# Four-layer conditioned sequence kernel: when the first batch's q and k, the heads' means, the first gates and the matrix exponential's pieces are issued

## The chip, the cores and the metric

One core of a Trainium2 chip. The metric is the device time of one execution in microseconds (us); the time of the kernel before is the median of 3 runs. Engines: TensorE (PE, with its weight loads PEld), VectorE (DVE), ScalarE (ACT), GpSimd (POOL) and SyncE (SP), which issues nearly all DMAs.

## The reference

Input x is 32 x 128 x 144 in float32, with a condition of 144 numbers for each of the 32 batches. Four layers follow one another:

- Layer L0 is a transformer block. From the condition come six vectors (shift, scale and gate, for attention and for the MLP). x is normalised, scaled and shifted; q, k and v are projected; **q and k are normalised over the 9 numbers of each of the 16 heads** (mean removed, divided by the root of the variance, times a gain); then softmax attention, projection, gated residual, and a gated MLP with gelu.
- Layer L1 rotates x in a 64-dimensional subspace: U comes from a QR factorisation of P (144 x 64), and the rotation is **the matrix exponential of a skew matrix** (64 x 64) that depends on the condition, one for each batch.
- Layer L2 is a transformer block as L0, without the normalisation of q and k.
- Layer L3 is one with a mixture of four experts, of which two are taken for each token.

```
qkv = xn @ w_qkv + b_qkv
...
q = _ln(q, g_q)
k = _ln(k, g_k)
attn = softmax(einsum('bhqd,bhkd->bhqk', q, k) * HD ** (-0.5))
...
U, _ = qr(P)
R = expm(A)
x_rot = x + einsum('btd,nd->btn', z @ R - z, U)
```

## The kernel before, in words

The kernel is written with the order of every engine's instructions given by hand. Time is cut into **ticks**; a tick is the work on one batch of 128 tokens in each of three stages. `at_tick` gives each batch of the three transformer layers its tick: batch b of L0 is at tick b, and layers L2 and L3 follow. In a tick the loop issues the scores of the current batch twice over (half the heads each, `scores`, L853), the exponentials of the batch before, and the weighting, division and projection of the batch before that (`weigh` L880, `sums`, `divide`, `project_out` L944). Between them lie named gaps, in this order: a, e, t, (scores, first half), stats, b0, b, den, pre1, (scores, second half), c, y1, y2, y3, d, z. `put(tick, gap, f, ...)` hangs other work into a gap, and `fill` issues it. A gap's work is issued in the order in which it was put there. Every engine takes its instructions in this order, so what waits holds up all that is behind it on that engine.

Ticks -6 to -1 are the lead-in: nothing is scored yet. What hangs in them and in the ticks of L0:

- `modulations(n)` (L274 to L281): 80 small matmuls and four DVE copies that make shifts and scales of layer n. `layer_gates(n)` (L291 to L298): eight matmuls, one ACT copy and two DMA writes of the gates to DRAM, from where `load_gates` (L305) reads them back for four batches at a time. `first_gates` is `layer_gates(0)` followed by two DMA loads of L3's modulation weights, over those of L0.
- `ln_stats` (L623 to L635): statistics of a batch on DVE and the normalised batch on POOL; `ln_T` (L652 to L655): its transposes on PE and the modulation on ACT.
- `qk0_project` (L686 and L687, ACT copies L741 and L742), `qk0_variance` (DVE L747, POOL L748), `qk0_guess` (DVE L754 and L757), three `qk0_newton` (L764 to L767: four small instructions, on POOL, for batch 0 on DVE), `qk0_divide` (DVE L771) and `qk0_T` (PE L783, ACT L786 to L788): q and k of one batch of L0. Batch i has its projection at tick i - 3, guess and Newton steps at i - 2, division and transposes at i - 1.
- `without_means` (L1166 to L1172): seven DVE instructions that take the mean over a head out of the weights of q and k once, so that the projection gives q and k without means.
- `prep_qr`: 64 columns of a Householder QR, three pieces each (PE L327, ACT L338 and L340, POOL L339; DVE L342 to L349; DVE L353). `prepare_qr` issues three pieces in a tick before 0 (e, then twice in stats) and six after it (a, twice in t, den, y1, y2): columns 6 and 7 fall into tick 0, 8 and 9 into tick 1.
- `prep_expm`: the exponential, cut into 50 pieces by `yield`: two pieces of modulations and gates for L2 and L3; four that make the skew matrices (L414, L420, L429, L434; the first of them issues four more loads of the weights W, L189); four for the norm and the number of squarings (L444 to L482); eight products for the powers (L501); two series of ten; two products; eight squarings (L561, L567); a branch L586 for more squarings, which is not taken here; a last subtraction (L592). `prepare_expm` issues one piece at the end of gap z of tick -2, and from tick 0 on one in b and one in z.
- When the QR and the exponential are done, `prep_rot` (L601) makes the rotations, and `load_late` issues the loads of the later layers' weights.

Of the kernel before, what the change touches and what calls it, by code (L numbers as in the profile page):

```python
# [66 lines left out]
def tile_kernel(ctx: ExitStack, tc: tile.TileContext, a: dict, out: bass.AP):  # L67
    nc = tc.nc
# [721 lines left out]
    def values(g, i0, n, rest_first=False):  # L790
        p = PARAMS[g[0]]
        if g[0] == 0:
            ps = by_token0(g, i0, n, p.wv, p.wvR, f"ps_v_{g[1]}")
            pss, copy = [ps.rearrange("p b c -> p (b c)")], nc.scalar.copy
        else:
            pss = yield from by_token(g, "a", i0, n, p.wv, p.wvR, f"ps_v_{g[0]}_{g[1]}", rest_first)
            copy = nc.vector.tensor_copy
        pair = take_v()
        for i in range(n):
            st[g[0] * B + g[1] * G + i0 + i]["v"] = pair[:, i * NH : (i + 1) * NH, :]  # L800

        m = 8 * n // len(pss)
        for i, ps in enumerate(pss):
            v = pair[:, 2 * m * i : 2 * m * (i + 1), :].rearrange("p (q r) s -> p q (r s)", r=2)
            src = ps.rearrange("p (q r d) -> p q r d", r=2, d=HD)
            copy(v[:, :, :HD], src[:, :, 0, :])
            copy(v[:, :, 48 : 48 + HD], src[:, :, 1, :])
# [353 lines left out]
    prep_qr, prep_expm = prep_qr(), prep_expm()  # L1161
# [41 lines left out]

    def prepare_expm(tick, gap):
        nonlocal prep_expm
        if prep_expm and (tick >= 0 and gap in ("b", "z") or (tick, gap) == (-2, "z")):
            said = next(prep_expm, 0)
            if said == 0:
                prep_expm = None
            elif said is not None:  # L1210
                rot_T.append(said)


    GAP = 3
    first = (0, B + GAP, 2 * B + GAP)
    at_tick = {first[l] + b: l * B + b for l in range(3) for b in range(B)}
# [3 lines left out]
    def put(tick, gap, f, *args):  # L1220
        gaps[tick, gap].append((f, args))

    def put2(tick, gap, to, f, *args):

        halves = []

        def first_half():
            halves.append(f(*args))
            next(halves[0])

        def second_half():
            for _ in halves[0]:
                pass

        put(tick, gap, first_half)
        put(tick, to, second_half)

    for layer in range(3):
        ahead = 5 if layer == 0 else 6
        for n in range(NG):  # L1240
            g = (layer, n)
            t0 = first[layer] + n * G
            for i in range(G):
                s = layer * B + n * G + i
                at_a = t0 + i - ahead
                if layer == 1 and n == 0:
                    at_a = t0 - 4 + i // 2
                if layer == 1 and i == 0:
                    put(at_a - 2, "d", rotate_T, n)
                    put(at_a - 1, "b", rotate_in, n)  # L1250
                    put(at_a - 1, "d", rotate, n)
                stats[at_a].append((s, "a"))
                stats[t0 + i + 3].insert(0, (s, "m"))
                if layer < 2:
                    put(*((at_a, "d") if at_a != t0 + i - ahead else (at_a + 1, "b")), ln_T, s, "a")
                else:
                    put(at_a, "d", ln_T, s, "a")
                if layer == 0:
                    put(t0 + i + 4, "a", ln_T, s, "m")
                else:  # L1260
                    put(t0 + i + 3, "d", ln_T, s, "m")
                if layer == 0:
                    put(t0 + i - 3, "c", qk0_project, s)
                    put(t0 + i - 3, "z", qk0_variance, s)
                    put(t0 + i - 2, "e", qk0_guess, s)
                    if s == 0:
                        for gap in "bbc":
                            put(-2, gap, qk0_newton, s, nc.vector)
                    else:
                        for gap in ("b", "c", "y2"):  # L1270
                            put(t0 + i - 2, gap, qk0_newton, s)
                    put(t0 + i - 1, "b", qk0_divide, s)
                    put(t0 + i - 1, "c", qk0_T, s)
            if layer == 0:
                for i in (0, 2):
                    put(t0 + i // 2, "b", lambda g=g, i=i: list(values(g, i, 2)))
            elif layer == 1:
                put2(t0, "stats", "b", values, g, 0, 2, True)
                put2(t0 + 1, "stats", "b", values, g, 2, 2, True)
            else:  # L1280
                put2(t0, "y2", "y2", values, g, 0, 2, True)
                put2(t0 + 1, "den", "pre1", values, g, 2, 2)
            if layer:
                put2(t0 - 2, "c", "c", qk_chunks, g)
                if g == (1, 0):
                    put(t0 - 2, "y2", qk_masked, g)
                for r in (1, 0):
                    if layer == 2 and n > 2:
                        for t in range(2):
                            put(t0 - 2 + (r == 0), "z", qk_mask, g, nc.gpsimd, t, r)  # L1290
                    elif g != (1, 0):
                        put(t0 - 1, "a", qk_mask, g, nc.gpsimd, 0, r)
                        put(t0 - 1, "b0", qk_mask, g, nc.scalar, 1, r)
            if layer == 0:
                put2(t0 + 10, "stats", "b", mlp1, g, 0, (0, 1, 2), True)
                put2(t0 + 11, "d", "d", mlp1, g, 3, (3, SHARED), False)
                for i in range(G):
                    put(t0 + 12 + i // 2, "bd"[i % 2], mlp2, g, i)
            elif layer == 1:
                put2(t0 + 8, "c", "c", mlp1, g, 0, (0, 1, 2), True)  # L1300
                put2(t0 + 9, "c", "c", mlp1, g, 3, (3, SHARED), True)
                for i in range(G):
                    put(t0 + (10, 10, 11, 11)[i], "bdbc"[i], mlp2, g, i)
            else:
                put2(t0 + 7, "den", "c", gate_logits, g)
                put(t0 + 8, "e", expert_ranks, g)
                put(t0 + 8, "stats", expert_weights, g)
                for i in range(G):
                    put(t0 + 8 + i // 2, "cdab"[i], moe_bias, g, i)
                for pair in range(2):  # L1310
                    at_ = t0 + 8 + 2 * pair
                    put2(at_, "stats", "b0", moe1, g, pair, 0, True)
                    put2(at_, "den", "pre1", moe1, g, pair, 1, False)
                    put2(at_ + 1, "stats", "b0", moe1, g, pair, 2, True)
                    put2(at_, "stats", "y1", shared_by_gate, g, pair)
                    put2(at_, "y2", "y3", moe2_parts, g, 2 * pair, 0)
                    put(at_ + 1, "b", moe2, g, 2 * pair, 1)
                    put(at_ + 1, "c", moe2, g, 2 * pair, 2)
                    put(at_ + 1, "y2", moe2, g, 2 * pair, 3)
                    for i in range(G):  # L1320
                        put(at_ + 2, "aabb"[i], moe2, g, 2 * pair + 1, i)
                put(t0 + 12, "b", moe_out, g)

    put(-5, "b", modulations, 0)
    put(-4, "b", first_gates)
    put(-4, "z", without_means)

    put(first[1] + B - 10, "c", load_L3)
    put(first[1] + B + 7, "d", lambda: load_pair(1, mlps[:, :PAIR_COLS]))
# [1 line left out]
    def fill(tick, gap):  # L1331
        prepare_qr(tick, gap)
        while (tick, gap) == (last_prep, "b0") and late is None:
            prepare_qr(tick, gap)
            prepare_expm(tick, gap)

        if gap == ("t" if tick < 0 else "e" if tick < first[1] else "stats") and tick in stats:
            ln_stats(stats.pop(tick))
        for f, args in gaps.pop((tick, gap), ()):
            f(*args)  # L1340
        prepare_expm(tick, gap)
# [213 lines left out]
```

## Time and profile before

| | us |
|---|---|
| median of 3 runs | 1320.95 (1320.02 to 1337.16) |
| the profiled execution's own time | 1327.05 |
| its span | 1325.3 |
| busy: PE, DVE, ACT, POOL | 1266.7, 799.8, 832.9, 699.9 |
| first scores (tick 0) begin | 40.88 |
| tick 3 begins | 72.77 |
| tick 25 begins | 336.25 |
| late weights are issued from | 395.23 |

Rows of the timeline read: start, duration, engine, line, operation, what is written and read, the shape, how many of the same are merged in the row; in brackets how long the engine stood idle before, and what released it. The table by stretches gives the busy time of PE, PEld, DVE, ACT and POOL in each, then the granted clock of TensorE (1 is full), then the DMA share and GB/s. A pass over a float32 matmul is two instructions, so a count of 2 is one product.

### The profile page before, as it was taken

The numbers are of one execution on the slowest core, as the hardware profiler recorded it, in microseconds if no ns is written. First come the engines' busy times: TensorE is split into PE (matmuls) and PEld (weight loads), VectorE is DVE, ScalarE is ACT, GpSimd is POOL, SyncE is SP. The second block draws the span as 40 slices with busy tenths as digits, with TensorE's granted clock in tenths as the row PEclk, the third lists the DMA queues.
The fourth block names the chain that finished last, engine by engine and source line by source line (L and its number), as shares of the span: only waits on it lengthen the run. The fifth ranks groups of instructions, "written<-read, shape, count | busy, mean of one in ns | idle before, by whom it ended". The sixth has DMA issues, their size and how long they took to land.

```text
span 1325.3 us, 35652 instructions
## 1 busy us (share of the span) xinstructions
PE 1266.7 (96%) x14180; PEld 923.5 (70%) x14180; DVE 799.8 (60%) x2516; ACT 832.9 (63%) x1832; POOL 699.9 (53%) x1691
## 2 busy tenths in 40 slices
PE   6989898999999989999999999999999999999997
PEld 5668686786776566677776766667676767677665
DVE  5698988866764355666566667545454546455322
ACT  2568767678767555686767777756565656555431
POOL 5667777756744343445445445736363636351632
PEclk9999999999999999999999999999999999999999
DMA  9200000000003000000110000201000000000000
GB/s 229 61 2 21 20 3 18 20 3 22 20 13 121 18 11 20 11 20 10 45 29 14 17 20 11 75 11 19 10 19 11 19 11 19 10 19 2 19 9 9
DMA packets 21671, 34.43 MB, mean 26 GB/s; under 512 B 2304, under 2 KB 12448, under 8 KB 21248
## 3 DMA queue, kind: packets, MB, share of 16 engines
q1 hardware_dynamic: 20848, 31.70, 8.0%
q8 instruction: 114, 1.87, 0.6%
q10 hardware_dynamic: 656, 0.42, 0.2%
q14 instruction: 53, 0.43, 0.1%
HBM read 29.65 MB, written 2.47 MB: 24 GB/s over the span
## 4 chain that ended last, share of the span: by engine, by line
PE 69%; DVE 4%; ACT 1%; issue 1%; POOL 0%; POOLq 0%; DVEq 0%
PE ps_h L665 19%; PE ps_f L1105 9%; PE ps_s L853 6%; PE ps_qk L665 6%; PE ps_o L880 5%; PE ps_w L853 5%; PE ps_f L970 4%; PE ps_pj L944 3%; PE ps_v L665 2%; DVE nm L858 2%; PE ps_f L1110 1%; PE ps_o L812 1%; PE ps_cw L1093 1%; PE ps_hT_m L652 1%; PE ps_hT_m L653 1%; PE ps_z L1002 1%
## 5 line engine op out<-in xcount | busy, mean ns | idle before, releaser
L858 DVE TENSOR_REDUCE nm<-ps_s 128x4 f32<-128x512 f32 x384 | 246.4, 682 | 96.9 <-PE ps_w L853 79.3
L865 ACT ACTIVATE pr<-ps_w 128x512 f32<-128x512 f32 x384 | 208.6, 595 | 107.6 <-PE ps_w L853 106.0
L853 PE MATMUL ps_w<-q,kT 32*128 32x128 f32 x3072 | 228.6, 283 | 0.2 <-ACT hid L964 0.2
L853 PE MATMUL ps_s<-kT,qT 32*128 32x256 f32 x1536 | 227.9, 404 | 0.7 <-ACT kT L788 0.6
L853 PEld LDWEIGHTS ps_w<-q,kT 32*128 32x128 f32 x3072 | 193.3, 186 | 9.7 <-issue 6.2
L964 ACT ACTIVATE hid<-ps_h 128x512 f32<-128x512 f32 (+1 forms) x224 | 119.1, 591 | 108.9 <-PE ps_h L665 108.5
L853 PEld LDWEIGHTS ps_s<-kT,qT 32*128 32x128 f32 x1536 | 134.9, 184 | 30.0 <-issue 9.2
L665 PE MATMUL ps_h<-hM_m,mlps 128*128 128x512 f32 x304 | 146.3, 615 | 0.0
L1114 DVE SCALAR_TENSOR_TENSOR acc<-ps_f,cw,acc 128x144 f32<-128x144 f32 x128 | 46.6, 366 | 152.3 <-PE ps_f L1110 73.6
L930 POOL TENSOR_TENSOR x_sb<-x_sb,res_a 128x144 f32<-128x144 f32 x96 | 47.0, 489 | 151.2 <-DVE res_a L933 149.9
L880 PE MATMUL ps_o<-pr,vaug 128*32 128x128 f32 x3072 | 104.9, 277 | 0.8 <-issue 0.8
L880 PEld LDWEIGHTS ps_o<-pr,vaug 128*32 128x32 f32 x3072 | 78.7, 110 | 34.3 <-PE ps_w L853 20.0
L665 PEld LDWEIGHTS ps_h<-hM_m,mlps 128*128 128x128 f32 x304 | 53.9, 191 | 66.2 <-issue 65.0
L731 POOL TENSOR_SCALAR kT<-kT,cst 128x512 f32<-128x512 f32 x40 | 62.3, 1563 | 61.6 <-ACT kT L718 60.6
L970 PE MATMUL ps_f<-mlps,hid 128*128 128x144 f32 x640 | 93.2, 293 | 0.0
L970 PEld LDWEIGHTS ps_f<-mlps,hid 128*128 128x128 f32 x640 | 82.5, 191 | 7.3 <-issue 3.4
L865 ACT ACT_TABLE_LOAD x57 | 73.1, 1283 | 8.0 <-PE ps_w L853 7.2
L626 POOL TENSOR_SCALAR rs_m_a<-mv_m_a 128x2 f32<-128x2 f32 x81 | 15.5, 191 | 116.6 <-DVE mv_m_a L624 88.2
L655 ACT ACTIVATE hM_m<-ps_hT_m,modM 128x128 f32<-128x128 f32 x96 | 44.6, 465 | 49.1 <-PE ps_hT_m L653 49.0
L961 ACT ACT_TABLE_LOAD x58 | 74.4, 1283 | 1.0
L930 POOL TENSOR_TENSOR x_sb<-x_sb,res_m 128x144 f32<-128x144 f32 x64 | 32.3, 510 | 80.0 <-DVE res_m L933 79.9
L1105 PEld LDWEIGHTS ps_f<-pair,hid 128*128 128x128 f32 x512 | 66.9, 190 | 8.4 <-issue 7.7
(324 smaller groups left out, 2963.5 us busy)
## 6 DMA issues: line engine op xcount, KB each, us to landing
gates<-gates SPq DMA_DIRECT2D x48, 288.0 KB, 3.5
x_sb<-in_x SPq DMA_DIRECT2D x8, 288.0 KB, 9.4
out_x<-x_sb SPq DMA_DIRECT2D x8, 288.0 KB, 2.5
mlps<-in_L_mlp SPq DMA_DIRECT2D x2, 1000.0 KB, 6.1
pair<-in_L_mlp SPq DMA_DIRECT2D x1, 1800.0 KB, 9.5
mlps<-in_L_mlp SPq DMA_DIRECT2D x1, 1800.0 KB, 8.2
pow<-in_W SPq DMA_DIRECT2D x4, 320.0 KB, 7.7
mlps<-in_L_wmod SPq DMA_DIRECT2D x4, 290.0 KB, 4.9
```

The source lines that it names most:

```text
L665: nc.tensor.matmul(ps, x, y, start=k == 0, stop=k == 1)
L731: eng.tensor_scalar(o, k, m, None, ALU.mult)
L853: nc.tensor.matmul(o, x, y, start=True, stop=True)
L858: nc.vector.tensor_reduce(nmv[:, at0 : at0 + 2, ONE : ONE + 2], view.rearrange("p (r t k) -> p r t k", t=2, k=T), AX.X, ALU.max, negate=True,)
L865: nc.scalar.activation(pr[:, 4 * e : 4 * e + 4, :].rearrange("p s q -> p (s q)"), view, AF.Exp, scale=SCALE,)
L880: nc.tensor.matmul(po[rows4(j), t, :], v[:, 4 * j + 2 * t + r, :], prs[j // 2][:, 4 * (j % 2) + 2 * r + t, :], start=r == 0, stop=r == 1,)
L930: nc.gpsimd.tensor_tensor(x_sb[:, b, :], x_sb[:, b, :], t, ALU.add)
L961: nc.scalar.activation(t, half, AF.Gelu_apprx_tanh)
L964: nc.scalar.activation(hid[:n, i], ps[:n], AF.Gelu_apprx_tanh)
L970: nc.tensor.matmul(ps, hid[:, at0, i, :], w2[:, m, :], start=m == 0, stop=m == NFC - 1)
L1105: nc.tensor.matmul(ps[:, 0, :], hid[:, at0 + m, i, :], w2[:, at0 + m, :], start=m == 0, stop=m == 3)
L1114: nc.vector.scalar_tensor_tensor(acc, ps[:, 0, :], w, acc, ALU.mult, ALU.add)
```

## The change

Batch 0's projection, variance, guess, Newton steps, division and transposes are each put one tick earlier (the transposes go before the other work of gap b of tick -2; the division into gap z of tick -3); those of the other batches stay. `without_means` goes from gap z of tick -4 to gap t of tick -5, after the first batch's statistics. `first_gates` goes from gap b of tick -4 to gap b0 of tick -2. The exponential's first piece is no longer issued at tick -2, nor the next ones in ticks 0 to 2: all begin at tick 3, two in a tick as before.

```
-        if prep_expm and (tick >= 0 and gap in ("b", "z") or (tick, gap) == (-2, "z")):
+        if prep_expm and tick >= FIRST_EXPM and gap in ("b", "z"):
...
+    FIRST_EXPM = 3
...
                 if layer == 0:
-                    put(t0 + i - 3, "c", qk0_project, s)
-                    put(t0 + i - 3, "z", qk0_variance, s)
-                    put(t0 + i - 2, "e", qk0_guess, s)
-                    if s == 0:
+                    early = s == 0
+                    put(t0 + i - 3 - early, "c", qk0_project, s)
+                    put(t0 + i - 3 - early, "z", qk0_variance, s)
+                    put(t0 + i - 2 - early, "e", qk0_guess, s)
+                    if early:
                         for gap in "bbc":
-                            put(-2, gap, qk0_newton, s, nc.vector)
+                            put(-3, gap, qk0_newton, s, nc.vector)
+                        put(-3, "z", qk0_divide, s)
+                        put(-2, "b0", first_gates)
+                        put(-2, "b", qk0_T, s)
                     else:
                         for gap in ("b", "c", "y2"):
                             put(t0 + i - 2, gap, qk0_newton, s)
-                    put(t0 + i - 1, "b", qk0_divide, s)
-                    put(t0 + i - 1, "c", qk0_T, s)
+                        put(t0 + i - 1, "b", qk0_divide, s)
+                        put(t0 + i - 1, "c", qk0_T, s)
...
     put(-5, "b", modulations, 0)
-    put(-4, "b", first_gates)
-    put(-4, "z", without_means)
+    put(-5, "t", without_means)
```

## The prediction

> **What bounds the kernel now.** I read the page's shares and slices, then the timeline of TensorE (PE) over the lead-in, then VectorE (DVE) over ticks 0 to 2, then the clock by stretches, then PE around tick 22.
>
> ```profile
> PE 1266.7 (96%) x14180; PEld 923.5 (70%) x14180; DVE 799.8 (60%) x2516; ACT 832.9 (63%) x1832; POOL 699.9 (53%) x1691
> PE   6989898999999989999999999999999999999997
> ```
> PE is busy 96% of the span; only the first of 40 slices (33 us each) stands at 6 tenths. Work can be moved, but PE's time can only shrink where it is idle or its clock is low.
>
> ```profile
> 16.86 2.13 PE L291 MATMUL ps_gate<-mlps,csT 72*32 72x144 f32 x8
> 24.95 1.17 PE L686 MATMUL ps_qk<-L_wqk,hM_a 128*128 128x288 f32 x2
> 37.46 1.09 PE L783 MATMUL ps_qkT<-cst,qkn 128*128 128x128 f32 x4 [3.01 <-DVE qkn L771]
> 40.88 1.55 PE L853 MATMUL ps_s<-kT,qT 32*128 32x256 f32 x8
> 43.66 2.56 PE L274 MATMUL ps_mod<-csT,mlps 72*128 72x32 f32 x74
> 49.14 0.65 PE L686 MATMUL ps_qk<-L_wqk,hM_a 128*128 128x288 f32 x2
> ```
> Columns: start, duration, engine, line, what, idle before it. The first scores come at 40.88, after 3.01 us of waiting for batch 0's division. The same 288-column pair takes 1.17 us before 41 us and 0.65 us after it: the lead-in runs at about half the clock. From 26.87 to 33.25 PE works on the exponential's first piece (modulations and gates of layer 1), 6.4 us at that speed.
>
> ```profile
> 42.67 0.16 DVE L342 SCALAR_TENSOR_TENSOR ala<-qrr,qr 128x1 uint32<-128x1 uint32 x1 [0.23 <-POOL qr L339]
> 53.96 0.16 DVE L342 SCALAR_TENSOR_TENSOR ala<-qrr,qr 128x1 uint32<-128x1 uint32 x1 [0.80 <-POOL qr L339]
> 64.37 0.16 DVE L342 SCALAR_TENSOR_TENSOR ala<-qrr,qr 128x1 uint32<-128x1 uint32 x1 [1.89 <-POOL qr L339]
> 75.44 0.15 DVE L342 SCALAR_TENSOR_TENSOR ala<-qrr,qr 128x1 uint32<-128x1 uint32 x1
> ```
> These four are the first QR column of ticks 0, 1, 2 and 3 on DVE, so those ticks last 11.29, 10.41 and 11.07 us.
>
> ```profile
> 76.00:80.00 4.00, 2.80 (x30) 2.18 (x31) 3.65 (x14) 1.34 (x6) 3.64 (x11) 0.91 0.00 0
> 80.00:84.00 4.00, 3.82 (x16) 2.40 (x14) 3.83 (x15) 2.38 (x6) 2.23 (x9) 0.66 0.00 0
> ```
> Third from the end is the granted clock: it drops after PE stood idle for 1.77 us before 77.20.
>
> ```profile
> 298.10 0.48 PE L853 MATMUL ps_s<-kT,qT 32*128 32x256 f32 x2
> 304.41 1.16 PE L561 MATMUL ps_sq<-pow 64*64 64x64 f32 x64
> 323.60 0.73 PE L944 MATMUL ps_pj<-L_wproj,oT 128*128 128x144 f32 x4 [1.24 <-PEq L586]
> 336.25 0.48 PE L853 MATMUL ps_s<-kT,qT 32*128 32x256 f32 x2
> 346.70 0.48 PE L853 MATMUL ps_s<-kT,qT 32*128 32x256 f32 x2
> 358.70 0.48 PE L853 MATMUL ps_s<-kT,qT 32*128 32x256 f32 x2
> ```
> Tick 22 starts at 298.10, tick 25 at 336.25, 26 at 346.70, 27 at 358.70. The exponential is over in tick 24 (its last subtraction is at 330.1), so ticks 25 to 27 run without pieces: 10.45, 12.0 and 11.4 us. The branch L586 costs PE 1.24 us.
>
> **The change part by part.** 50 pieces (a 51st call ends the generator) now run one at tick -2 and two per tick from 0; afterwards two per tick from 3, ending at 28.
>
> *Means (tick -4 to -5).* Seven DVE instructions from 19.33 to 21.71, 2.38 us. They now start at about 10.9, after the first statistics; their weights, issued at 3.34 and 4.29, landed 5.9 and 5.3 us later. QR column 1 on DVE slips from 12.53 to 13.3 and ends at 15.1. Cost nothing: PE is in the first modulations until 15.73. Without that cover it is 0.8 us.
>
> *Gates (tick -4 to -2).* Eight matmuls, 2.13 us on PE, one ACT copy of 0.39, two DMA writes and two weight loads on SP. SP is busy with x loads until 25.44 and writes the gates at 25.56 now; later it is about 27.5, and the loads about 29 instead of 26.87. The first reader, the gates' load issued at 34.56, has until tick 2; the weights until tick 3. On PE they fall into a wait for DVE. Nothing, or 2.1 us where PE was not waiting.
>
> *Batch 0's q and k.* Batch 0's h is ready at 17.87, so the projection runs 17.7 to 19.85 instead of 20.70 to 23.19, its variance is done on DVE at 21.1. Guess, QR column 3 (to 24.1), three Newton steps (0.88 each, as from 27.57 to 30.1 now) and division end at 27.2 instead of 37.3. Queued behind them on DVE is QR column 4: 27.75 instead of 25.90. PE: gates to 26.9, transposes 27.3, projection of batch 1 28.6 to 30.7, column 5, projection of batch 2 to 33.7. Column 5 ends on DVE at 35.0, and scores could start at 35.7 instead of 40.88. But POOL is next: batch 1's three Newton steps (1.30 us each, as from 37.46 to 41.28 now) start at 35.3 and end at 39.2, and the root of column 6 is queued behind them. DVE's column 6 thus comes at 40.5 instead of 42.67. Gain 2.2 us; ends: 0 (if POOL starts no earlier) and 5.2 (scores' own gain).
>
> *Ticks 0 to 2 lose their pieces.* Tick 0 sheds 3.5 us of modulations (43.66 to 47.14) and 1.85 us of W on PE; what stays on PE is 6.4 us. DVE stays busy 8.5, 8.5 and 8.0 us, less 0.9 of copies, 1.05, and 1.05 with the 1.21 row sum. With the QR chain's wait of 0.5 to 1 us I take 8.8 us a tick: 26.5 against 32.77, gain 6.3. Ends: 8 us (DVE alone, 8.2 a tick) and 2 us (10.3 a tick, with PE at half clock for a good half of each).
>
> *Clock.* PE stands idle in these ticks now, about 2 us each. The row says 1.77 us idle cost a stretch in which the clock lost 0.09 and 0.34 of 4 us, 1.7 us. One such drop: +1.5; ends 0 and 4 (a drop in nearly every tick).
> [...]
>
> *The pieces in ticks 3 to 28.* Seven pieces that ran before tick 3 now run in it or later: on PE 3.48 twice, 1.85, 1.16, 2.7, 1.16, together 13.8 us. I laid each tick's new pair on a tick of the same phase. Ticks 3 to 7: PE or DVE sets 14.5, 11.9, 11.5, 11.6 and 10.5 us against 12.52, 10.63, 10.47, 9.55 and 9.47, that is +7.3. Ticks 8 to 24: pairs change places among alike ones, -1.3. Ticks 25 to 27: squarings as in ticks 21 and 22 (12.95 and 13.30) and the branch, against 10.45, 12.0 and 11.4: +2.5, +1.3, +1.2. Sum 11.0. Ends: 8 (PE's idle time in ticks 25 to 28, about 5 us, takes them) and 14 (all of it on the path).
>
> *Branch.* L586 moves from the end of tick 23 to the middle of tick 27, where PE is further ahead of DVE; queued behind it are values, scores and all the rest of the tick. +1; ends 0 and 3.
>
> **Sum.** -2.2 - 6.3 + 1.5 + 11.0 + 1.0 = +5.0 us. The profiled execution took 1327.05 (span 1325.3 and 1.75 around it), so its like would take 1332; it stood 6.1 above the median of the runs shown, 1320.95. On that median: **1326 us**.
>
> **Rivals.**
> *The filler costs nothing later.* The pieces of ticks 25 to 28 and 3 to 7 run in idle time: the last sum is 8 less 1, the branch 0, the clock 0: -8.5 + 7 = -1.5, and with DVE-bound ticks 0 to 2 (8 us) and the scores' 5.2: -6. Time 1315 to 1320. For: PE idles 2.7 us in tick 28 and 2.1 in tick 3. Against: tick 25 has PE busy for all of its 10.45.
> *Half clock through ticks 0 to 2.* Speaks for it: the lead-in's 9 us of unbroken PE work from 23.88 to 33.25 did not lift the clock, and the ticks after hold less work. At half clock 6.5 us of work a tick become 13: 39 against 32.77 is +6.2 where I counted -4.8; sum +16, 1337. Against: the clock did lift at about 42.
> *Slower by over 2%.* The exponential outlives the QR tail, and the late weights, issued from 395.23, come late. It now ends at tick 28; the QR tail ends there too, so one piece more begins to delay. A squaring in a row costs about 3.6 us (PE, ACT and PE again), so from eight such pieces on it is over 26 us. Count from the row at 330.1: none is left. 1350.
> *Nothing moves at the head.* POOL's Newton steps hold column 6 at 42.67: +2.2 more, 1328.
>
> **How the numbers follow.** Forecast 0.53 (its own range 1321 to 1331), no cost later 0.25, half clock 0.15, nothing at the head 0.05, late weights 0.02. The range leaves out less than 2 in 10: down to 1314 for the first rival, up to 1337 for half clock; single runs of the same kernel already lie between 1320.02 and 1337.16. 2% is 26 us, about what a measurement of this kernel can tell from no change: faster 0.01 (a tail of the first rival), slower 0.02, within 0.97.
>
> **What would show it.** Batch 0's projection near 18 and its transposes near 27; first scores near 36; column 6 on DVE near 40.5; ticks 0 to 2 near 9 us; tick 3 over 14 us with 7 us of modulations; squarings up to tick 26 and tick 25 near 13 us; the branch's wait on PE in tick 27. Wrong it would be if ticks 0 to 2 stay above 10.5 us, if ticks 25 to 27 do not grow, or if the time moves in layers 1 and 2, which the change does not touch.

## The result, and the profile after

The changed kernel takes 1336.73 us (median of 20 runs, 1332.64 to 1342.63), the kernel before, run beside it, 1327.13 (20 runs, 1320.02 to 1337.16). The ratio of their runs is 1.0060 with a 95% interval of [1.0041, 1.0079], about +8.0 us (the medians lie 9.6 apart). Predicted were +5.0. The 1326 of the prediction stood on 1320.95, the median of three runs; twenty runs put the kernel before 6.2 us higher, so the change is what is compared here, not the time itself. The profiled execution took 1336.78 against 1327.05: +9.7.

The page of the changed kernel, busy time of the engines, then PE in 40 slices (33 us each):

```profile
PE 1267.7 (95%) x14180; PEld 925.5 (69%) x14180; DVE 800.8 (60%) x2516; ACT 833.0 (62%) x1832; POOL 703.1 (53%) x1691
...
PE   5798998899989998999999999999999999999997
```

PE's busy time over the whole span grew by only 1.0 us; the page alone would say that nothing happened. The first slice is emptier (5 for 6). The loss has to be looked for by stage.

The head first. PE's timeline of the changed kernel over the lead-in (start, duration, engine, line, what, idle before):

```profile
17.09 1.33 PE L686 MATMUL ps_qk<-L_wqk,hM_a 128*128 128x288 f32 x2 [0.64 <-DMA x_sb<-in_x]
...
26.48 1.11 PE L783 MATMUL ps_qkT<-cst,qkn 128*128 128x128 f32 x4
...
34.42 1.13 PE L853 MATMUL ps_s<-kT,qT 32*128 32x256 f32 x8
41.21 0.82 PE L327 MATMUL ps_qr<-at,cst 128*128 128x145 f32 x2 [4.26 <-DVE at L353]
```

Batch 0's projection, transposes and scores come at 17.1, 26.5 and 34.4 (worked out: 17.7, 27.3, 35.7). But the scores' gain of 6.5 us is not kept. PE then waits 4.26 us for column 6 of the QR, and that waits for POOL. DVE's timeline of the changed kernel, first its wait ahead of column 6:

```profile
38.69 0.18 DVE L754 TENSOR_SCALAR qky<-qkv 128x32 int32<-128x32 int32 x1 [3.97 <-POOL qkv L748]
39.32 0.16 DVE L342 SCALAR_TENSOR_TENSOR ala<-qrr,qr 128x1 uint32<-128x1 uint32 x1 [0.24 <-POOL qr L339]
49.20 0.16 DVE L342 SCALAR_TENSOR_TENSOR ala<-qrr,qr 128x1 uint32<-128x1 uint32 x1 [0.24 <-POOL qr L339]
57.68 0.16 DVE L342 SCALAR_TENSOR_TENSOR ala<-qrr,qr 128x1 uint32<-128x1 uint32 x1 [0.23 <-POOL qr L339]
66.83 0.14 DVE L342 SCALAR_TENSOR_TENSOR ala<-qrr,qr 128x1 uint32<-128x1 uint32 x1
```

Batch 1's Newton steps hold POOL from 34.5 to 38.4, DVE stands for 3.97 us, and column 6 comes at 39.32, 3.35 us sooner than before (predicted 40.5, 2.2 sooner). The next three lines are the first columns of ticks 1, 2 and 3: ticks of 9.88, 8.48 and 9.15 us, 27.5 in all where they took 32.8.

Then the stretches: ticks 0 to 2, 3 to 28, 29 to 43, by their starts on PE. Columns: length, busy PE, PEld, DVE, ACT, POOL, granted clock, DMA share, GB/s. The kernel before:

```profile
40.88:72.77 31.89, 30.45 (x399) 21.76 (x398) 24.99 (x87) 19.03 (x58) 18.86 (x62) 1.00 0.22 53
72.77:385.32 312.55, 292.66 (x4106) 231.39 (x4105) 254.93 (x874) 231.81 (x625) 216.47 (x614) 0.99 0.04 14
385.32:573.68 188.36, 175.47 (x1917) 123.44 (x1915) 97.06 (x278) 115.28 (x234) 77.60 (x190) 0.96 0.10 34
```

The changed kernel:

```profile
34.42:65.19 30.77, 23.45 (x214) 17.50 (x213) 22.12 (x79) 17.52 (x53) 21.87 (x73) 0.89 0.00 1
65.19:399.66 334.47, 313.75 (x4378) 247.36 (x4377) 259.36 (x887) 233.90 (x629) 217.06 (x614) 0.96 0.06 18
399.66:583.12 183.46, 170.55 (x1918) 120.44 (x1916) 96.56 (x277) 115.18 (x234) 77.94 (x190) 0.99 0.10 35
```

Tick 3 begins 7.6 us sooner, ticks 3 to 28 are 21.9 longer, and ticks 29 to 43 4.9 shorter. That last gain is no step of the change: the instructions there are the same, and the clock is at half speed for 3.4 us instead of 13.7. So a good part of the difference between two single profiles is where the clock happened to fall, and the size of the result is taken from the repeated runs.

In ticks 3 to 28 PE has 272 instructions more. Its idle time (length less busy) is 19.9 us before and 20.7 after: **on balance no idle time was filled**. (Without PE's wait at the branch, shown below, it is 18.7 and 17.1, so 1.6 us were filled.) All 21.1 us of the additional busy time lengthen the stretch. Of these 13.8 are the seven moved pieces as the prediction's rows price them; the remaining 7.3 go with 17.1 us more at half clock (at half clock, 8.5 us of work take 17.1).

One of these drops begins in tick 27. PE in the changed kernel, then the stretch behind the wait:

```profile
364.88 0.70 PE L853 MATMUL ps_s<-kT,qT 32*128 32x256 f32 x4
371.63 0.82 PE L327 MATMUL ps_qr<-at,cst 128*128 128x145 f32 x2 [3.64 <-PEq L586]
382.11 0.48 PE L853 MATMUL ps_s<-kT,qT 32*128 32x256 f32 x2
```

```profile
372.00:376.00 4.00, 4.00 (x33) 3.44 (x33) 1.63 (x4) 1.51 (x5) 2.41 (x9) 0.50 0.02 6
```

The branch L586 costs PE 3.64 us here (1.24 before), and behind the wait the clock stands at 0.50: tick 27 takes 17.24 us instead of 11.41.

The branch instruction itself is no longer than before. Its rows on TensorE's sequencer (the duration in ns, three times, as there is one of it; then where it starts), before and after:

```profile
L586 PEldq COMPARE_BRANCH  x1: 3823/3823/3823, 319.5 to 319.5; - x1
```

```profile
L586 PEldq COMPARE_BRANCH  x1: 3763/3763/3763, 367.6 to 367.6; - x1
```

It runs beside the products that PE still has to do. Before, PE had work until 322.36, so of the 3.8 us only the end was a wait; after, its work ended at 367.99, just after the branch had begun. In both profiles the branch takes 45 to 76 ns on each other engine. What fills the 3.8 us on TensorE no run shows.

### The profile page after: what moved, and what is told of

It reads as the page before. It is cut to its first block, busy times and chain, and to the rows that moved or that the text cites. A ratio compares the mean times of both kernels' runs of the same rounds, so it can differ in the third digit from the quotient of the medians.

```text
span 1335.1 us, 35656 instructions
## 1 busy us (share of the span) xinstructions
PE 1267.7 (95%) x14180; PEld 925.5 (69%) x14180; DVE 800.8 (60%) x2516; ACT 833.0 (62%) x1832; POOL 703.1 (53%) x1691
## 4 chain that ended last, share of the span: by engine, by line
PE 66%; DVE 4%; ACT 1%; POOL 1%; issue 1%; POOLq 0%; DVEq 0%
PE ps_h L665 18%; PE ps_f L1105 9%; PE ps_s L853 6%; PE ps_qk L665 6%; PE ps_o L880 5%; PE ps_w L853 5%; PE ps_f L970 4%; PE ps_pj L944 3%; PE ps_v L665 2%; DVE nm L858 2%; PE ps_f L1110 1%; PE ps_o L812 1%; PE ps_cw L1093 1%; PE ps_z L1002 1%; PE ps_hT_m L653 1%; PE ps_hT_m L652 1%
## 5 line engine op out<-in xcount | busy, mean ns | idle before, releaser
L853 PE MATMUL ps_s<-kT,qT 32*128 32x256 f32 x1536 | 231.6, 408 | 0.6 <-ACT kT L788 0.6
L626 POOL TENSOR_SCALAR rs_m_a<-mv_m_a 128x2 f32<-128x2 f32 x81 | 15.6, 193 | 115.8 <-DVE mv_m_a L624 87.5
```

The lines of the kernel that those rows point to most:

```text
L853: nc.tensor.matmul(o, x, y, start=True, stop=True)
```

## The experiments

Each kernel was timed in 12 runs beside 35 of the kernel before (medians 1326.7 to 1328.2). The expectations call theories by letters: D, the deferral of the pieces is the cost; L, the moves in the lead-in are; B, the branch in its new place adds to it; C, the low clock in ticks 0 to 2 does; P, the loss lies with the first piece, as long as it isn't in tick -2.

**The deferral alone** (the kernel before with the new start).

```
-        if prep_expm and (tick >= 0 and gap in ("b", "z") or (tick, gap) == (-2, "z")):
+        if prep_expm and tick >= 3 and gap in ("b", "z"):
```

> The kernel before with only the exponential's start moved to tick 3. Theory D (the deferral costs: seven pieces leave a lead-in that had room and land in ticks where TensorE is full): ticks 3 to 28 grow by about 20 us as in the changed kernel, ticks 0 to 2 and the head give back 6 to 9; +9 to +13 us on the kernel before. Theory L (the lead-in half costs, by its idle PE and its half clock in tick 0): within 3 us of the kernel before.

Measured: 1338.58 us, 1.0067 [1.0038, 1.0096]; ticks 3 to 28 take 335.3 us. The whole loss is there without the rest of the change.

**The lead-in alone** (the changed kernel with the old start).

```
-        if prep_expm and tick >= FIRST_EXPM and gap in ("b", "z"):
+        if prep_expm and (tick >= 0 and gap in ("b", "z") or (tick, gap) == (-2, "z")):
```

> The changed kernel with the exponential's pieces at their old places (one at tick -2, two a tick from 0); the rest of the lead-in as changed. Theory D: -2 to -5 us on the kernel before, from a shorter head; ticks 3 to 28 as before. Theory L: +5 us or more.

Measured: 1324.83 us, 0.9981 [0.9950, 1.0011]: not told from no change, and no loss. L falls. The parts add up: -0.19% and +0.67% make +0.48%, where both together measured +0.60% [0.41, 0.79].

**All pieces from tick 0** (one piece fewer in the lead-in, all later ones half a tick later).

```
-    FIRST_EXPM = 3
+    FIRST_EXPM = 0
```

> The changed kernel with the exponential begun at tick 0 instead of 3: the branch then falls into gap b of tick 24. Theory D without a special cost of the branch: -2 to -5 us on the kernel before. Theory B (the branch in the middle of a tick costs a stall of about 3.6 us on PE and then a half clock of 3.4 to 6.8 us): a stall of 3 us or more in tick 24, and 0 to +4 us on the kernel before.

Measured: 1334.47 us, 1.0048 [1.0021, 1.0076], about +6. That is dearer than one piece should be, the more so as the piece that crosses the start of tick 3 here, the row sum L444, has no work on PE. PE's wait at the branch is 1.99 us, in tick 24, which takes 14.21 us for 11.53. Its profile also has half clock from 34.5 to 51.6, and tick 0 lasts 20.9 us. Ticks 0 to 2 in its stretches:

```profile
34.44:77.72 43.28, 42.59 (x486) 31.83 (x486) 24.63 (x89) 19.49 (x57) 21.67 (x73) 0.76 0.17 41
```

This is the "half clock through ticks 0 to 2" of the rivals, here for a part of them and with PE busy 42.59 of 43.28 us. It set in after a stretch with waits (31.12 to 34.53, PE busy 1.44 of 3.41 us), but idle time did not keep it there. Its runs spread from 1329.9 at a mean clock of 0.986 to 1338.9 at 0.978.

**The branch in another gap** (all pieces half a tick later).

```
-        if prep_expm and tick >= FIRST_EXPM and gap in ("b", "z"):
+        if prep_expm and tick >= FIRST_EXPM and gap in ("b", "z") and (tick, gap) != (3, "b"):
```

> The changed kernel with all pieces half a tick later (the first in gap z of tick 3), so that the branch falls into gap z of tick 27, as it stood at the end of tick 23 in the kernel before. Theory B: the stall is 1.2 us instead of 3.64, tick 27 is 13.5 us instead of 17.2, and the time is 4 to 6 us under the changed kernel's. Theory D alone: within 2 us of the changed kernel.

Measured: 1332.34 us, 1.0041 [1.0016, 1.0066]. PE's timeline of this kernel in tick 27:

```profile
361.94 0.70 PE L853 MATMUL ps_s<-kT,qT 32*128 32x256 f32 x4
374.27 0.73 PE L944 MATMUL ps_pj<-L_wproj,oT 128*128 128x144 f32 x4 [1.43 <-DVEq L586]
375.39 0.48 PE L853 MATMUL ps_s<-kT,qT 32*128 32x256 f32 x2
```

The wait is 1.43 us instead of 3.64 and the tick 13.46 instead of 17.24, though it has a squaring more. So B, that the branch's new place adds to the cost, holds for this tick. Gap z alone does not make the branch cheap: in the two kernels with fewer pieces put off, below, it stands in gap z as well (of ticks 25 and 26), and PE waits 2.60 and 3.88 us for it. In whole times the gain over the changed kernel is 4.4 us by medians and 2.5 by ratios, and the intervals overlap.

**No branch, after and before.** Both kernels leave out the further squarings and the branch that guards them, a part of the computation.

```
-        n_more = nc.values_load(more, min_val=0, max_val=1)
-        with tc.If(n_more > 0):
-            for t in range(NSQ1, NSQ):
-                for _ in square(t):
-                    pass
```

> The changed kernel without the branch and the further squarings behind it (left out; they are not taken with these inputs). Theory B (the branch in mid-tick is what the sum had too small): the 3.64 us stall of tick 27 and the half clock after it go, 4 to 7 us under the changed kernel, about 1.001 to 1.003 of the kernel before. Theory D alone (the deferred work itself): 1 to 2 us under the changed kernel.

> The kernel before without the branch and the further squarings (left out). Both theories: the stall of 1.24 us at the end of tick 23 goes, 0 to 2 us under the kernel before. The gap between this and the changed kernel without the branch is the price of the deferral alone: D says 5 us or more, B says 3 us or less.

Measured: 1332.40 us, 1.0045 [1.0019, 1.0070], and 1324.29, 0.9995 [0.9964, 1.0026]. The gap between the two is the change without a branch: 0.5% or 6.6 us by the ratios (8.1 by medians), with an interval of about ±5 us from the two together. With the branch the loss was 8.0 us. By these values most of the loss is there without the branch, which is the smaller term; its share, 1.4 us, is not told from nothing.

**Filler in tick 0** (six products that nobody reads, to keep the clock up).

```
+    def filler():
+        ps = bank([128, 3, C], "ps_fill")
+        for _ in range(6):
+            nc.tensor.matmul(ps, ident, x_sb[:, :3, :], start=True, stop=True)
+
+    put(0, "b", filler)
```

> The changed kernel with six products of 128 x 432 on TensorE added in gap b of tick 0, whose result nobody reads (about 3.6 us at full clock), where PE stood idle for 4.26 us. Theory C (the idle stretch costs by the half clock that follows it): tick 0 falls from 13.0 to about 11 us in the profile, the time is 1 to 3 us under the changed kernel. Theory W (only the wait for POOL costs, and the clock nothing): tick 0 stays at 13 us or grows, the time is the same within 1 us.

Measured: 1335.47 us, 1.0063 [1.0036, 1.0090]. Its PE timeline, and ticks 0 to 2 in its stretches:

```profile
36.47 4.52 PE L1335 MATMUL ps_fill<-x_sb,cst 128*128 128x432 f32 x12
40.87 0.48 PE L327 MATMUL ps_qr<-at,cst 128*128 128x145 f32 x2
```

```profile
34.11:63.12 29.01, 25.02 (x226) 17.99 (x225) 22.00 (x79) 17.43 (x53) 21.87 (x73) 1.00 0.00 1
```

C, that the wait in tick 0 costs clock, is right in its place: with the wait of 4.26 us filled (by 4.52 us of products, where about 3.6 were expected), the QR product takes 0.48 instead of 0.82 us, the clock is full and tick 3 begins 2.1 us sooner (0.3 of it from an earlier first score). The whole time does not show it, and its interval of ±3.6 us could hide so little; the bulk of the loss is not there.

**Fewer pieces put off.** Start in gap z of tick 1 (four pieces moved behind the start of tick 3), and the first piece back in tick -2 with the others from tick 3 (six moved).

```
-        if prep_expm and tick >= FIRST_EXPM and gap in ("b", "z"):
+        if prep_expm and tick >= FIRST_EXPM and gap in ("b", "z") and (tick, gap) != (1, "b"):
...
-    FIRST_EXPM = 3
+    FIRST_EXPM = 1
```

> The changed kernel with the pieces begun in gap z of tick 1: two ticks earlier than with a start in gap z of tick 3, and the branch at the end of tick 25. Theory D: each piece put off costs about 1 us, so 2 to 5 us under the kernel begun in gap z of tick 3, and 0 to 3 us over the kernel before. Theory B alone: the same as with a start in gap z of tick 3, within 2 us, as the branch stands at the end of a tick in both.

```
-        if prep_expm and tick >= FIRST_EXPM and gap in ("b", "z"):
+        if prep_expm and (tick >= FIRST_EXPM and gap in ("b", "z") or (tick, gap) == (-2, "z")):
```

> The changed kernel, with the exponential's first piece back at the end of tick -2 and the other 49 from tick 3 on. Theory D in its plain form (each of the seven deferred pieces costs about 1 us): 1 to 2 us under the changed kernel, 1.004 to 1.005 of the kernel before. Theory P (it is the first piece's place, where TensorE waits for DVE and runs at half clock anyway, that was given away): most of the loss goes, 1.000 to 1.002.

Measured: 1332.14 us, 1.0052 [1.0023, 1.0081], and 1332.04, 1.0037 [1.0012, 1.0061]. P falls: with its first piece in place the kernel still loses. The whole times do not grow with the number of pieces. The stretch that takes them does; from the tables by stretches, one profile each, ordered by the pieces moved past the start of tick 3:

| kernel | moved | tick 3 starts | ticks 3 to 28 | PE busy in them | clock |
|---|---|---|---|---|---|
| before | 0 | 72.77 | 312.55 | 292.66 | 0.99 |
| before, no branch | 0 | 79.62 | 310.57 | 291.87 | 0.99 |
| lead-in alone | 0 | 80.51 | 314.66 | 296.13 | 0.97 |
| from tick 0 | 1 | 77.72 | 319.62 | 297.95 | 0.97 |
| from tick 1, z | 4 | 72.28 | 320.78 | 298.80 | 0.99 |
| one, then from 3 | 6 | 68.55 | 325.67 | 304.59 | 0.97 |
| after, no branch | 7 | 64.84 | 326.14 | 307.99 | 0.98 |
| after, filler | 7 | 63.12 | 332.74 | 312.16 | 0.97 |
| after | 7 | 65.19 | 334.47 | 313.75 | 0.96 |
| deferral alone | 7 | 63.80 | 335.34 | 315.04 | 0.96 |
| branch in gap z | 7 | 65.98 | 326.60 | 308.37 | 0.98 |

The length of ticks 3 to 28 follows PE's busy time nearly one to one: their difference is 18 to 22 us in every row. What is put there is paid there, and the clock decides the rest. What the head gains is less. (The three starts of tick 3 near 80 us belong to executions with half clock in the head.)

**A version that beats both?** In the profile of the lead-in alone DVE still waits 3.27 us for POOL ahead of column 6. Two edits on top of it: batch 1's Newton steps on DVE, and the first piece one tick earlier; then both.

```
-                            put(t0 + i - 2, gap, qk0_newton, s)
+                            put(t0 + i - 2, gap, qk0_newton, s, nc.vector if s == 1 else nc.gpsimd)
```

> The kernel with the lead-in changed and the exponential at its old places, and batch 1's three Newton steps on DVE instead of POOL, where DVE waits 3.3 us for them before tick 0. Theory: column 6 of the QR comes about 1.3 us earlier; 0.996 to 0.999 of the kernel before. If POOL is not what holds the head: the same as the lead-in alone, 0.998.

```
-        if prep_expm and (tick >= 0 and gap in ("b", "z") or (tick, gap) == (-2, "z")):
+        if prep_expm and (tick >= 0 and gap in ("b", "z") or (tick, gap) == (-3, "z")):
```

> The kernel with the lead-in changed and the exponential at its old places, but its first piece at the end of tick -3, where PE stands idle for 3.1 us, instead of tick -2. Theory P: the piece takes the idle time there and delays QR column 4 by 1 to 2 us, and tick -2 is 6 us shorter: 0.994 to 0.997 of the kernel before. Rival: POOL and DVE hold the head all the same, and the gain is under 2 us: 0.997 to 0.999.

> Both of these together: the first piece at the end of tick -3 and batch 1's Newton steps on DVE. If they act on different waits, the gains add: 0.992 to 0.996 of the kernel before; if on the same wait, the better of the two alone.

Measured: 1321.88 us, 0.9955 [0.9927, 0.9982]; 1324.74, 0.9978 [0.9950, 1.0005]; 1326.81, 0.9982 [0.9956, 1.0009]. DVE's timeline of the kernel with the first edit:

```profile
38.87 0.19 DVE L764 TENSOR_TENSOR qkh<-qkv,qky 128x32 f32<-128x32 f32 x1
41.06 0.16 DVE L342 SCALAR_TENSOR_TENSOR ala<-qrr,qr 128x1 uint32<-128x1 uint32 x1 [0.23 <-POOL qr L339]
```

The Newton steps are now part of DVE's own row of work and the wait for POOL is gone. It is the one kernel here that is faster than before, by 6 us. It is not shown to be faster than the lead-in alone (the intervals overlap), and with the first piece moved as well the gain is not seen: those gains do not add, and why was not settled.

## Why the prediction was right, and where its sizes were off

- **Sign and place: right.** It was a trade of some 7 us at the head against more behind it, and the time went up: +8.0 measured [about +5.4 to +10.5 by the interval], +5.0 predicted. By the ratios of the two halves the lead-in's moves are -2.5 us (interval -6.6 to +1.5; -2.2 predicted) and the deferral +8.9 (+5.0 to +12.8; its terms in the sum make +7.2).
- **Batch 0's q and k: right.** Of the scores' 6.5 us only 3.35 reach column 6, as POOL's Newton steps hold it; 2.2 had been taken. Of the difference 0.5 is that the first data came that much sooner in this execution (QR column 0 begins on PE at 6.39, before at 6.87).
- **Ticks 0 to 2: right.** 5.3 us gained on DVE, 4.8 expected with the clock's 1.5 in it. The drop was twice as long as the one counted, 6.8 us at half clock for 3.4 (a loss of 1.7), but it did not cost twice as much: the tick with it took 9.88 us, the two at full clock 8.48 and 9.15, where 8.8 each were worked out before the clock's term. Without the lead-in's first piece the head came to the full clock sooner, in these two profiles: a 288-column pair takes 1.17 us at 27.82 and 0.65 at 30.23 in the changed kernel, and still 1.17 at 39.30 in the kernel before.
- **Means and gates: nothing, as said.** PE's steps of the lead-in came 0.5 to 1.3 us before the worked out times, so neither held the path.
- **The pieces in ticks 3 to 28: right in kind, mis-sized.** With the branch's 1 us, +12.0 was taken for this stretch; in the profile it grew by 21.9. Where the clock stayed full the tick by tick sum held: ticks 25 and 26 grew by 2.5 and 1.3 us, as worked out, and ticks 4 to 6 took 34.4 (35.0 worked out). The excess stands in the ticks with half clock: tick 3 took 15.6 us (14.5 worked out), tick 7 12.5 (10.5), tick 27 17.2 (13.6 with the branch's 1) and tick 28 17.5 (15.2). Ticks 8 to 24 together changed by 0.1 (-1.3). Of the 9.9 us beyond the sum, 7.3 are PE's work at half clock, 1.4 the branch, and 1.2 the credit for PE's idle time: that idle time was to take 2.8 us of the pieces (13.8 less 11.0), and it took 1.6. In the two kernels without a branch it took 0.55 (18.70 us of idle time before, 18.15 after). Most of it is waits for DVE, and a piece that stands elsewhere in PE's order does not fall into them.
- **Branch: mis-sized, for another reason than the one given.** +1 was taken, as PE would be further ahead of DVE; the wait grew by 2.4 us (within the ends of 0 and 3), and half clock for 6.8 us followed it. What grew is neither the branch (3.82 us on TensorE before, 3.76 after) nor a wait for DVE: in the changed kernel DVE is at the branch at 368.9 us and through at 370.1, while TensorE is at it from 367.6 to 371.4, and PE's wait there is what the work in front of it leaves uncovered.
- **Clock: the term that was missing.** One drop was counted, for ticks 0 to 2. None was counted for ticks 3 to 28, where the profile has 23.9 us at half clock instead of 6.8. Part of that is chance: in ticks 29 to 43 the changed kernel has 10.2 us less of it than the kernel before. Over the runs the mean clock is 0.988 before and 0.984 after, but that mean takes the head as full up to the first change on record, 41.8 us in the profile before and 29.8 in the one after, so it does not price the stretch.
- **The rivals.** "Costs nothing later" fell: the deferral alone costs as much as the whole change. "Nothing moves at the head" fell. The late weights fell: they are issued from 409.55, 14.3 us later, which is just what tick 29 starts later. "Half clock through ticks 0 to 2" is not in the changed kernel's profile, but it is, for 17 us, in that of the kernel that starts at tick 0: it does occur, but there in ticks that are as full as before.

**What stays open:** starting all pieces at tick 0 costs 6 us, as much as four, six or seven pieces put off, and the intervals of ±3 us do not separate these; so the price of a piece is read from the stretches of single profiles and not from whole times.

## What to carry to other kernels

Work that fills a lead-in is cheap there, where the engine that bounds the kernel waits anyway; put off into a stretch where that engine is over 90% busy, it cost nearly its full duration in the profiles here, though that stretch showed idle time. Before idle time is counted as a gain, ask which instruction stands in the engine's order in front of each wait, and whether the moved work stands behind it. The run-time branch took TensorE 3.82 us in the profile before and 3.76 in the one after: its price there was what of that time the work queued on PE in front of it did not cover, a wait of 1.24 and of 3.64 us. In the other kernels whose wait is given above it was 1.43 to 3.88 us.

## What the runs showed of the hardware

**A wait of the same length cost clock in one profile and none in the other.** Around 214 us both kernels wait 2.45 us for the same product. Before (timeline, then stretches):

```profile
213.82 0.48 PE L327 MATMUL ps_qr<-at,cst 128*128 128x145 f32 x2 [2.44 <-DVE at L353]
```

```profile
212.00:216.00 4.00, 2.18 (x32) 1.93 (x33) 3.76 (x12) 1.05 (x5) 3.64 (x10) 1.00 0.01 4
```

After:

```profile
214.49 0.82 PE L327 MATMUL ps_qr<-at,cst 128*128 128x145 f32 x2 [2.45 <-DVE at L353]
```

```profile
212.00:216.00 4.00, 1.55 (x9) 1.20 (x12) 3.69 (x15) 1.45 (x6) 3.59 (x10) 0.76 0.01 2
```

Before, the clock stays at 1.00 through the wait; after, it falls in that stretch (0.76 is its mean), and the product takes 0.82 instead of 0.48 us. All drops in the two profiles but the last, at their very end, are 3.4 or 6.8 us long, once or twice the same length. They also start whole multiples of 3.413 us apart within a profile: before, at 79.3, 164.7 and 451.4 us, 25 and 84 times that length; after, at 40.0, 70.8, 122.0 and 214.1 us, 9, 15 and 27 times. Counted on from the drops in steps of that length, a step before ends at 212.44 and splits its wait into 1.1 and 1.4 us, while after, 2.1 us of the wait lie in the step that ends at 214.11, where the clock falls. Whether the place of a wait among these steps decides, no run tried, and the share of busy time in a step does not settle alone what follows: 2.11 us busy of 3.41 (75.90 to 79.31, before) were followed by half clock, 2.04 of 3.42 (212.44 to 215.86, before) were not. Waits of 1.77 us (before, ahead of 77.20) and 1.83 (after, ahead of 120.37) ended 2.1 and 1.6 us before a drop began, and the one of 2.45 (after) 0.4 us after it had.

**PE was busy and stood at half clock all the same.** In the profile of the lead-in alone the clock is at half speed from 24.6 to 58.7 us, with PE nearly always busy, much of it with products 32 columns wide:

```profile
45.55 4.49 PE L274 MATMUL ps_mod<-csT,mlps 72*128 72x32 f32 x78
```

The same loop takes 2.56 us for 74 in the kernel before. Such a drop follows the moved pieces in tick 3 of the changed kernel: PE is busy all through the 3.41 us before it, from 67.58 to 70.6 us with the first piece's modulations, and then stands at half clock:

```profile
67.34:70.75 3.41, 3.41 (x93) 3.30 (x90) 3.10 (x12) 1.25 (x4) 3.05 (x10) 1.00 0.00 0
70.76:74.16 3.40, 3.40 (x30) 2.62 (x29) 0.68 (x4) 0.94 (x4) 1.37 (x5) 0.50 0.06 16
```

The deferral alone has the same, with PE busy from 65.6 to 69.0 us and half clock for 6.8 us after it. In the changed kernel with the filler, and in the one without the branch, tick 3 has the same work, no drop, and takes 14.06 us instead of 15.61. What in this work brings the drop no run shows: none changed the width of its products alone. The execution of the lead-in alone that was profiled took 1335.19 us, while the median of that kernel is 1324.83; such a stretch at the head may be what makes runs of one kernel differ by 10 us. The clock column does not always tell it: in the kernel before without a branch, whose head has the old order, 78 of these products take 4.50 us at 45.58 and a 288-column pair 1.17 us at 55.58, as at half clock, while the column reads 1.00 in every stretch from 40 to 80 us. In a lead-in the clock is read from the length of a known product.
